# A two-layer adaLN stack: rows gathered by a token table instead of scattered by slot, and every engine in program order

## The chip, the cores and the metric

The kernel runs on one core of a Trainium2 chip. Its time is the device time in microseconds (us) of one execution; before the change the median of nine runs is 735.34 us (732.69 to 738.86). The profile is of one further execution. The core's engines run side by side, each through its own queue of instructions: PE (matrix products, and PEld, its weight loads), DVE and ACT (elementwise work, reductions, activations), POOL (elementwise work and all indirect DMAs here) and SP (which here only starts DMAs). They wait for each other by semaphores.

## The reference

8 sequences of 256 tokens with 128 channels, float32, go through two layers of adaptive layer norm. In each layer a token mixer and a mixture of experts are added to x, each with its own shift, scale and gate for each sequence:

```python
h = _layernorm(x) * (1 + ca) + sa
x = x + ga * attn(h)          # layer 0: retention, layer 1: softmax attention
h = _layernorm(x) * (1 + cb) + sb
x = x + gb * ffn(h)           # both: 8 experts, each token goes to 2
```

Layer 0's mixer is retention: causal scores with a decay for each head, 16 heads of 8 channels, rotary positions, a group norm over the channels of a head and all positions of a sequence, and a silu gate. Its experts are relu(x W1 + b1) W2 + b2, with 512 hidden channels. Layer 1's mixer is softmax attention within chunks of 256 tokens, which is one sequence. Its experts are (silu(x G) * (x U)) D. The two chosen experts' outputs are weighted by a softmax over their two router logits.

## The kernel before

**Tiling.** The 2048 tokens are 4 groups of 512 (`G`, `NTL` = 4 tiles of 128 tokens), resident in SBUF as `xg[g]`. The mixers work group by group and chunk by chunk: `retention` (L581) for layer 0, `Attention` (L767, `run` L973) for layer 1. The experts work on halves of two groups: 1024 tokens, `HT` = 8 tiles. With two choices for each token there are 2048 rows, which are sorted by expert into `NS` = 23 blocks of 128 slots; each expert's rows begin at a block's first slot, so that every block has one expert and some slots are empty.

**A half's way through the experts.** `route` (L343) normalises x into `hm` (`modulated_norm`, DVE L268, POOL L277 and L278), forms router logits on PE, takes the top two on DVE, counts the tokens of each expert by a triangular product (pc, L395) and so obtains for each token and choice its slot (`slot`, L426) and for each block its expert (`ex`). It then writes the 16 tiles of rows (8 tiles, two choices) to a DRAM buffer `xs` at their slots: 16 indirect DMAs on POOL (L447), each of 128 rows of 512 bytes. `xs` has 23 × 128 rows and is filled with zeros at the start by two DMAs (L110), since empty slots are read too. `experts` (L457) reads `xs` back in plain loads of four blocks (`fetch`, L466, on SP's queue), transposes four blocks at a time on PE (`turn`, L469, pt_s L244; ACT copies the result to xT, L474), and for each block loads its expert's weights (`we`, L501, on SP's queue, the expert's number read from `ex` into a register), computes the hidden channels (`hidden0` L741: PE ph, ACT and DVE h; `hidden1` L998: PE pg and pu, ACT sg, DVE h L1010), and one block later the output (`leave`, L477: py on PE L480, DVE copy yr L485). Every four blocks go to the DRAM buffer `ys` by a store on ACT's queue (L488). `combined` (L514) brings each token's two result rows back by two indirect DMAs on POOL (yk, L536; 16 for each half), weights and adds them (ACT L540, DVE L543), in layer 0 adds the b2 term by PE, and `add_gated` (L308) multiplies by the gate on DVE and adds to x on POOL (x L316). After layer 1 a group leaves by a store on SP's queue (L1045).

**Order.** Side work is written as Python generators in a list, `sides`. `tick` (L182) moves each of them on to its next `yield`. The main loops call `tick` two or three times in each block or round, so that routing, combining and the modulation's matmuls are emitted between the main instructions. `tc.manual_schedule(engines={PE})` (L1013) keeps PE's instructions in the order in which they are emitted; the instructions of DVE, ACT, POOL and SP are put in order by a scheduler.

**Which halves meet what.** Routing of half 0 of layer 0 runs beside retention, that of half 1 beside experts(0,0). `combined(0,0)` and the attention's projections run beside experts(0,1), `combined(0,1)` and routing of layer 1's half 0 beside attention, routing of half 1 beside experts(1,0), `combined(1,0)` beside experts(1,1), and `combined(1,1)` alone at the end.

Of the kernel before, what the change touches and what calls it, by code (L numbers as in the profile page):

```python
# [10 lines left out]
FP = mybir.dt.float32  # L11
# [7 lines left out]
P = 128  # L19
# [23 lines left out]
def kernel(  # L43
# [59 lines left out]

    xs, ys = [], []
    zeros = wk.tile([P, P], FP, tag="rs", name="zeros", bufs=1)
    nc.gpsimd.memset(zeros, 0.0)
    for half in range(G // HG):
        xs.append(tc.dram_tile([NS * P, C], FP, name=f"xs{half}"))
        ys.append(tc.dram_tile([NS * P, C], FP, name=f"ys{half}"))
        nc.sync.dma_start(  # L110
            out=xs[half].rearrange("(j p) c -> p j c", p=P),
            in_=zeros.unsqueeze(1).to_broadcast([P, NS, P]),
        )
# [36 lines left out]
                   allow_small_or_imprecise_dtypes=True)  # L150
    slot_no = const.tile([P, NS, NE], FP, tag="slot_no", name="slot_no")
# [34 lines left out]

    def settle():
        while sides:
            tick()


    def modulation(layer, c_sb, wmod_sb, made):
# [13 lines left out]
        scb = wk.tile([P, B, P], FP, tag="hm", name=f"scb{layer}")  # L206
        nc.vector.tensor_copy(scb, sc.unsqueeze(2).to_broadcast([P, B, P]))
# [3 lines left out]
        for b in range(0, B, 2):  # L211
            yield
            pg = bank("sc", f"pg{layer}_{b}")
            for n in range(2):
                nc.tensor.matmul(
                    pg[:, n * 256 : (n + 1) * 256], lhsT=scb[:, b + n, :],
                    rhs=wmod_sb[:, 4:6, :], start=True, stop=True,
                )
# [11 lines left out]
            for n in range(2):  # L230
                nc.tensor.matmul(
                    pr[:, n * 256 : (n + 1) * 256], lhsT=scb[:, b + n, :],
# [21 lines left out]
    def modulated_norm(key, g, mod, shift, scale, got, rows=None, hm=None):  # L254
# [4 lines left out]
        for t in range(NTL):  # L259
            nc.vector.bn_stats(st[:, t, :], xg[g][:, t, :])  # L260
        for t in range(NTL):
            nc.vector.bn_aggr(mv[:, t, :], st[:, t, :])
        rstd = inv_std(key, mv[:, :, 1], NTL)
        yield
        yield
        xn = wk.tile([P, NTL, P], FP, tag="xn", name=f"xn_{key}")
        for t in range(NTL):
            nc.vector.tensor_scalar(  # L268
                xn[:, t, :], xg[g][:, t, :], mv[:, t, 0:1], rstd[:, t : t + 1],
                ALU.subtract, ALU.mult,  # L270
            )
        if rows is not None:
            for n in range(2):
# [5 lines left out]
        yield  # L279
        yield  # L280
# [9 lines left out]
        yield  # L290
# [17 lines left out]
    def add_gated(key, g, gates, which, y):  # L308

        tmp = wk.tile([P, NTL, P], FP, tag="t3", name=f"res_{key}", bufs=1)  # L310
# [32 lines left out]
    def route(layer, half, ready, wr, bias):  # L343
# [6 lines left out]
        hm = wk.tile([P, HT, P], FP, tag="hm", name=f"hm_{key}")  # L350
        lg = sm.tile(sh, FP, tag="lg", name=f"lg_{key}")
        mx = sm.tile(sh, FP, tag="mx", name=f"mx_{key}")
        mi = sm.tile(sh, U32, tag="mi", name=f"mi_{key}")
        for u in range(HG):
# [5 lines left out]
            yield from modulated_norm(f"{key}_{u}", g, mod, SB, CB, got, rows, hm[:, tiles, :])  # L360
# [3 lines left out]
            for t in range(NTL):  # L364
                nc.tensor.matmul(
                    pv[:, t, :], lhsT=hT[:, t * P : (t + 1) * P], rhs=wr, start=True, stop=True
                )
            if bias is None:
# [18 lines left out]
        both = sm.tile([P, HT + 1, NE], BF, tag="both", name=f"both_{key}")  # L387
        nc.gpsimd.memset(both[:, HT, :], 0.0)
        nc.vector.tensor_tensor(both[:, :HT, :], pick[:, 0], pick[:, 1], ALU.add)
        yield  # L390
        yield
# [8 lines left out]
        pos = sm.tile([P, HT + 1, NE], FP, tag="pos", name=f"pos_{key}")  # L400
        nc.vector.tensor_copy(pos, pc)

        big = sm.tile([P, NE, NE], FP, tag="big", name=f"big_{key}")
# [10 lines left out]
        at_slot = sm.tile(sh, FP, tag="lg", name=f"as_{key}")  # L414
# [12 lines left out]

        past = wk.tile([1, NS, NE], FP, tag="past", name=f"past_{key}", bufs=1)
# [7 lines left out]
        w = sm.tile([P, 4, HT], FP, tag="w2", name=f"w2_{key}")  # L436
        d, e = w[:, 2, :], w[:, 3, :]
        nc.vector.tensor_tensor(d, mx[:, :, 1], mx[:, :, 0], ALU.subtract)
        nc.scalar.activation(e, d, AF.Exp)
        nc.vector.tensor_scalar(d, e, 1.0, None, ALU.add)  # L440
        nc.vector.reciprocal(w[:, 0, :], d)
        nc.vector.tensor_tensor(w[:, 1, :], e, w[:, 0, :], ALU.mult)
        own = []
        for t in range(HT):
            yield
            for k in range(2):
                inst = nc.gpsimd.indirect_dma_start(  # L447
                    out=xs[half][:, :],
                    out_offset=bass.IndirectOffsetOnAxis(ap=slot[:, k, t : t + 1], axis=0),
                    in_=hm[:, t, :], in_offset=None,  # L450
                )
                for other in own:
                    tc.declare_no_dep(inst.ins, other, reason="no two choices share a slot")
                own.append(inst.ins)
        routed[layer, half] = (slot, w, pick, ex)

    def experts(layer, half, blob, width, hidden):  # L457


        _, _, _, ex = routed[layer, half]  # L460
        xs_view, ys_view = (a[half].rearrange("(j p) c -> p j c", p=P) for a in (xs, ys))

        def fetch(q):
            n = min(NTL, NS - q)
            xr = wk.tile([P, NTL, P], FP, tag="xr", name=f"xr_{layer}_{half}_{q}", bufs=3)
            nc.sync.dma_start(out=xr[:, :n, :], in_=xs_view[:, q : q + n, :])  # L466
            return xr

        def turn(q, xr):  # L469
# [683 lines left out]
```

## Time and profile before

| what | value |
|---|---|
| median of nine runs | 735.34 us |
| profiled execution | 733.37 us |
| its span, first to last instruction | 731.7 us |
| mean granted TensorE clock | 0.855 |
| DMA, mean over the span | 122 GB/s, 89.22 MB |
| retention (0 to 131.4 us) | PE busy 98.84 us |
| experts(0,0) (144.7 to 236) | PE busy 73.22 us |
| experts(0,1) (236 to 325) | PE busy 67.62 us |
| attention (325 to 521) | PE busy 155.01 us |
| experts(1,0) (521 to 611) | PE busy 77.24 us |
| experts(1,1) (611 to 698.5) | PE busy 69.52 us |

The page has the busy time of each engine; the span in 40 slices, in which a digit is the busy share in tenths, PEclk the granted clock of PE in tenths of full speed; DMA queues; the chain of work that ended last; and groups of instructions by line, with their count, busy time, mean duration and the idle time of the engine ahead of them, by what ended it (`<-`). Views of the trace give the same for chosen windows, the waits by pair, and a timeline of single instructions. In a name such as `yk_c<-ys,slot_r` the output stands first, then the inputs.

### The profile page before, as it was taken

Reading aid. Unit: us, or ns where it says so; the run is one execution under the profiler, and the core shown is the slowest. Engines: PE = TensorE matmul, PEld = TensorE weight load, DVE = VectorE, ACT = ScalarE, POOL = GpSimd, SP = SyncE. Lnnn points to the kernel's source line nnn. Section 1 sums busy time; section 2 is a strip of 40 time slices with the busy share of each in tenths; the row PEclk is TensorE's granted clock in tenths of the full one; section 3 lists DMA queues with packets and bytes.
Section 4 is the critical chain, followed back from the end, with each engine's and each line's share of the span. In section 5 each row is a group of like instructions: output and inputs, shape, how many; then the busy total and the mean of one; then the engine's idle time right before and its main releaser. Section 6 shows DMA issues by size and latency. Waiting matters only on the chain.

```text
span 731.7 us, 12589 instructions
## 1 busy us (share of the span) xinstructions
PE 541.5 (74%) x4608; PEld 407.6 (56%) x4608; DVE 340.5 (47%) x1053; ACT 225.7 (31%) x495; POOL 296.5 (41%) x418
## 2 busy tenths in 40 slices
PE   3899784197588589938786997858997697489910
PEld 2555452096587567814443453425797697479910
DVE  5566665264233476423767576825362231233311
ACT  1553341142123342423352443412441121212201
POOL 5457466835305430065335136475126202600045
PEclk9999897589698799965898798966998799599975
DMA  8300004256585246610000000430176598378712
GB/s 239 98 22 1 2 1 138 79 172 219 172 267 164 85 144 183 204 44 25 1 2 1 1 3 1 147 127 3 46 259 236 194 299 296 96 248 303 260 36 61
DMA packets 53902, 89.22 MB, mean 122 GB/s; under 512 B 5576, under 2 KB 39248, under 8 KB 53840
## 3 DMA queue, kind: packets, MB, share of 16 engines
q1 hardware_dynamic: 37584, 73.99, 31.3%
q0 software_dynamic: 4096, 8.40, 3.8%
q10 hardware_dynamic: 12160, 6.03, 2.8%
q8 instruction: 36, 0.59, 0.3%
q14 instruction: 26, 0.21, 0.1%
HBM read 74.11 MB, written 14.29 MB: 121 GB/s over the span
## 4 chain that ended last, share of the span: by engine, by line
PE 41%; DVE 15%; POOL 14%; DMA 14%; issue 10%; another core or an unknown queue 3%; ACT 2%; SPq 0%; POOLq 0%; ACTq 0%; DVEq 0%
DMA we<-in_l_ew_dram 8%; PE py L480 8%; DVE nm L850 5%; POOL yk_c L536 4%; PE pg L1003 4%; PE sm L844 4%; PE ph L747 4%; PE pu L1003 4%; DMA yk_c<-ys,slot_r 2%; DMA ys<-yr 2%; POOL xs L447 2%; PE sm L836 2%; PE pn L939 2%; POOL x L316 2%
## 5 line engine op out<-in xcount | busy, mean ns | idle before, releaser
L480 PE MATMUL py<-we,h 128*128 128x128 f32 x736 | 105.9, 290 | 27.4 <-DVE h L1010 14.6
L536 POOL DMA_INDIRECT yk_c<-ys,slot_r x64 | 61.3, 958 | 157.1 <-DMA ys<-yr 136.9
L480 PEld LDWEIGHTS py<-we,h 128*128 128x128 f32 x736 | 96.5, 204 | 33.2 <-DVE h L1010 15.3
L447 POOL DMA_INDIRECT xs<-hm_r,slot_r x64 | 62.5, 977 | 47.6 <-DVE slot_r L426 30.3
L850 DVE TENSOR_REDUCE nm<-sm 128x4 f32<-128x512 f32 x96 | 60.2, 680 | 17.7 <-PE sm L844 17.4
L1010 DVE TENSOR_TENSOR h<-pu,sg 128x512 f32<-128x512 f32 x46 | 31.7, 689 | 78.0 <-PE pu L1003 58.3
L903 ACT ACTIVATE e<-se 128x512 f32<-128x512 f32 x96 | 49.9, 600 | 55.1 <-PE se L897 50.2
L320 POOL TENSOR_SCALAR_AFFINE_SELECT e<-e 128x512 f32<-128x512 f32 x64 | 39.7, 643 | 59.9 <-ACT e L903 59.8
L1003 PE MATMUL pg<-xT,we 128*128 128x128 f32 x368 | 52.8, 289 | 11.9 <-DMA we<-in_l_ew_dram 5.6
L747 PE MATMUL ph<-xT,we 128*128 128x128 f32 x368 | 54.0, 294 | 6.7 <-DMA we<-in_l_ew_dram 3.4
L1003 PEld LDWEIGHTS pg<-xT,we 128*128 128x128 f32 x368 | 47.2, 201 | 15.1 <-ACT xT L474 6.6
L1008 ACT ACTIVATE sg<-pg 128x512 f32<-128x512 f32 x46 | 27.4, 596 | 90.5 <-PE pg L1003 72.4
L747 PEld LDWEIGHTS ph<-xT,we 128*128 128x128 f32 x368 | 49.0, 206 | 10.6 <-DMA we<-in_l_ew_dram 5.2
L1003 PE MATMUL pu<-xT,we 128*128 128x128 f32 x368 | 51.8, 285 | 0.5 <-issue 0.3
L755 DVE TENSOR_SCALAR h<-ph,we 128x128 f32<-128x128 f32 x92 | 28.2, 344 | 46.6 <-ACT h L753 16.7
L753 ACT ACTIVATE h<-ph,we 128x128 f32<-128x128 f32 x92 | 28.7, 365 | 68.5 <-PE ph L747 30.9
L1003 PEld LDWEIGHTS pu<-xT,we 128*128 128x128 f32 x368 | 47.6, 202 | 0.9 <-issue 0.9
L543 DVE SCALAR_TENSOR_TENSOR acc_c<-yk_c,w_r,acc_c 128x128 f32<-128x128 f32 x32 | 11.2, 351 | 77.1 <-DMA yk_c<-ys,slot_r 74.8
L844 PE MATMUL sm<-kz,qs_a 32*128 32x512 f32 x192 | 40.4, 745 | 0.0
L485 DVE COPY yr<-py 128x128 f32<-128x128 f32 x92 | 26.5, 288 | 27.6 <-PE py L480 14.6
L540 ACT ACTIVATE acc_c<-yk_c,w_r 128x128 f32<-128x128 f32 x32 | 12.9, 402 | 77.0 <-DMA yk_c<-ys,slot_r 73.4
L320 POOL TENSOR_SCALAR_AFFINE_SELECT a<-a 128x512 f32<-128x512 f32 x32 | 20.6, 658 | 25.6 <-ACT a L648 25.6
(199 smaller groups left out, 932.9 us busy)
## 6 DMA issues: line engine op xcount, KB each, us to landing
we<-in_l_ew_dram SPq DMA_DIRECT2D x46, 768.0 KB
we<-in_l_ew_dram SPq DMA_DIRECT2D x46, 514.0 KB
xr<-xs SPq DMA_DIRECT2D x20, 256.0 KB
ys<-yr ACTq DMA_DIRECT2D x20, 256.0 KB
xs<-zeros SPq DMA_DIRECT2D x2, 1472.0 KB
x<-in_x_in_dram SPq DMA_DIRECT2D x4, 256.0 KB
xs<-hm_r,slot_r POOLq DMA_INDIRECT x64
yk_c<-ys,slot_r POOLq DMA_INDIRECT x64
```

The costliest lines, as they stand in the source:

```text
L320: nc.gpsimd.affine_select(out=src, in_=src, compare_op=ALU.is_ge, fill=0.0, base=0, pattern=[[0, 4], [1, P]], channel_multiplier=-1,)
L447: inst = nc.gpsimd.indirect_dma_start(out=xs[half][:, :], out_offset=bass.IndirectOffsetOnAxis(ap=slot[:, k, t : t + 1], axis=0), in_=hm[: ...
L480: nc.tensor.matmul(py, lhsT=h[:, fc, :], rhs=we[:, width - FF + fc * C : width - FF + (fc + 1) * C], start=(fc == 0), stop=(fc == NFC - 1),)
L536: nc.gpsimd.indirect_dma_start(out=yk[:, k, :], out_offset=None, in_=ys[half][:, :], in_offset=bass.IndirectOffsetOnAxis(ap=slot[:, k, at ...
L747: nc.tensor.matmul(ph[:, i, :], lhsT=we[:, fc * P : (fc + 1) * P], rhs=xT, start=True, stop=True)
L753: nc.scalar.activation(h[:, fc, :], ph[:, i, :], AF.Relu, bias=b1)
L755: nc.vector.tensor_scalar(h[:, fc, :], ph[:, i, :], b1, 0.0, ALU.add, ALU.max)
L844: nc.tensor.matmul(scs[i], lhsT=qs[part, t0 : t0 + P], rhs=kz[part, :, k * P : (k + 1) * P], start=(k != c), stop=True,)
L850: nc.vector.tensor_reduce(nm[:, 4 * i : 4 * i + 4], scs[i], AX.X, ALU.max, negate=True)
L903: nc.scalar.activation(e, scs[i], AF.Exp)
L1003: nc.tensor.matmul(p[:, fc, :], lhsT=we[:, i * FF + fc * P : i * FF + (fc + 1) * P], rhs=xT, start=True, stop=True,)
L1010: nc.vector.tensor_tensor(h, pu, sg, ALU.mult)
```

## The change

1. *Rows.* `xs` now holds the 1024 tokens in their order (`HT` × 128 rows). `route` stores `hm` there, a plain store of four tiles for each group on POOL's queue. The zero fills are gone. A **token table** says for each slot which token's row belongs there. It is built on chip: the slot is split into a block number (`part[:, 0]`) and a row in the block (`part[:, 1]`); `owner` holds, for each token, choice and block, the token's row and tile number where the token's slot lies in that block, and zero elsewhere (three DVE operations of 128x368); `hot` is, for each tile and choice, a 128x128 bf16 matrix that has a one at the row of the slot (16 DVE operations), and 16 matmuls add `hot`ᵀ × `owner` into `pown` (128x46). Two DVE operations make of it `token` (row + 128 × tile). An empty slot gets token 0.
2. *Gathers.* Each block's rows come by an indirect DMA on POOL from `xs` by `token[:, j]` (23 for each half, 92 in all) in place of the scatters and of `fetch`. For the first half of a layer the first eight are issued in `begun`, one for each stage; later ones one for each block, eight blocks ahead, running over into the first eight of the half that follows.
3. *Order.* `tc.manual_schedule()` without an argument: DVE, ACT, POOL and SP too run in the order in which instructions are emitted. The side generators yield much more often (`hop`), retention ticks four times instead of two or three for each chunk, and attention five times instead of three for each round.
4. *Routing's place.* The routes of both halves of a layer are started together and run side by side (`routing`), with two buffers for several small tiles. `hm` becomes one tile for each group.
5. *Combining.* `combined` begins three stages later. The rows of tile `at` are gathered two tiles ahead of the arithmetic on them, the two gathers in separate stages. `add_gated` multiplies in place there.
6. *Queues.* The out stores move from SP's to POOL's queue. The `ys` stores (still ACT's queue) are issued one step later, after the next block's hidden products. The modulation's broadcast `scb` is made for four sequences at a time.

```diff
-        own = []
-        for t in range(HT):
-            yield
-            for k in range(2):
-                inst = nc.gpsimd.indirect_dma_start(
-                    out=xs[half][:, :],
-                    out_offset=bass.IndirectOffsetOnAxis(ap=slot[:, k, t : t + 1], axis=0),
-                    in_=hm[:, t, :], in_offset=None,
-                )
...
+            nc.gpsimd.dma_start(
+                out=xs[half].rearrange("(u t p) c -> u p t c", p=P, t=NTL)[u], in_=hm
+            )
...
+        nc.vector.tensor_tensor(
+            owner[:, 1], block.unsqueeze(1).unsqueeze(1).to_broadcast(per),
+            part[:, 0].unsqueeze(3).to_broadcast(per), ALU.is_equal,
+        )
+        nc.vector.tensor_scalar(owner[:, 0], owner[:, 1], token_row[:, 0:1], None, ALU.mult)
+        nc.vector.tensor_tensor(
+            owner[:, 1], owner[:, 1], token_tile.unsqueeze(3).to_broadcast(per), ALU.mult
+        )
...
+                    nc.vector.tensor_scalar(
+                        hot, row16, part[:, 1, k, t : t + 1], None, ALU.is_equal
+                    )
...
+                    nc.tensor.matmul(
+                        pown, lhsT=hots[2 * (t - 2) + k], rhs=owner[:, :, k, t - 2, :],
+                        start=(t == 2 and k == 0), stop=(t == HT + 1 and k == 1),
+                    )
...
+    def gather(layer, half, j):
+
+        q, t = j // NTL, j % NTL
...
+        nc.gpsimd.indirect_dma_start(
+            out=raw[layer, half, q][:, t, :], out_offset=None, in_=xs[half][:, :],
+            in_offset=bass.IndirectOffsetOnAxis(ap=token[:, j : j + 1], axis=0),
+        )
...
+    def begun(layer, half):
+
+        for j in range(2 * NTL):
+            gather(layer, half, j)
+            yield
...
-        raw = {0: fetch(0), NTL: fetch(NTL)}
...
+            for _ in range(2):
+                if ahead and ahead[0][:2] in routed and total - len(ahead) <= j:
+                    gather(*ahead.pop(0))
...
             tick()
+            store()
             if last is not None:
                 leave(*last)
             tick()
...
-    with tc.manual_schedule(engines={mybir.EngineType.PE}):
+    with tc.manual_schedule():
...
-            nc.sync.dma_start(out=out_view[g], in_=xg[g])
+            nc.gpsimd.dma_start(out=out_view[g], in_=xg[g])
```

More of the change, by code (lines that the diff above doesn't have):

```diff
@@ L455, in route @@
[L455 to L469, printed above, removed]
-            n = min(NTL, NS - q)
+        per = [P, 2, HT, NS]
@@ L475, in turn @@
             return xT
+        full = []
         def leave(j, we, h, yr):
@@ L508, in experts @@
             tick()
[L509 to L510 removed]
+            if j % NTL == 2 and (q + 1) * NTL < NS:
+                xT[q + 1] = turn(q + 1)
             last = (j, we, h, yr)
         leave(*last)
+        store()
+        for more in ahead:
+            while following not in routed:
+                tick()
+            gather(*more)
     def combined(layer, half, finished):
         key = f"c{layer}_{half}"
[L518 removed]
+        slot, w, pick, _, _ = routed[layer, half]
+        yield from hop(3)
         gates = made[layer][1]
```

264 lines of the change are left out of this document (170 added, 94 removed).

## The prediction, made before the changed kernel had run

> **What bounds the kernel now.** The page's first two parts come first: no engine is full, PE is the fullest.
>
> ```profile
> span 731.7 us, 12589 instructions
> PE 541.5 (74%) x4608; PEld 407.6 (56%) x4608; DVE 340.5 (47%) x1053; ACT 225.7 (31%) x495; POOL 296.5 (41%) x418
> PE   3899784197588589938786997858997697489910
> POOL 5457466835305430065335136475126202600045
> PEclk9999897589698799965898798966998799599975
> ```
>
> Each digit is 18.3 us. PE's digits fall to 1 (slice 8) and about 5 (10, 13, 31), where POOL's rise; its clock falls with its work. So I asked next for busy time by windows around POOL's long runs of indirect DMAs: three of scatters, three of gathers, a stretch of comparison, the boundary before layer 0's experts and the tail.
>
> ```profile
> core 0: us, PE busy (x) PEld busy (x) DVE busy (x) ACT busy (x) POOL busy (x), PEclk, DMA share, GB/s
> 170.40:190.50 20.10, 10.37 (x74) 9.29 (x74) 3.49 (x14) 2.46 (x7) 15.46 (x16) 0.85 0.51 168
> 470.80:488.80 18.00, 8.74 (x74) 4.68 (x74) 5.38 (x13) 1.97 (x5) 14.12 (x15) 0.80 0.49 185
> 551.80:571.90 20.10, 11.22 (x86) 10.23 (x84) 2.16 (x5) 2.38 (x4) 15.49 (x16) 0.79 0.54 183
> 225.00:245.00 20.00, 10.45 (x48) 8.34 (x47) 6.04 (x16) 6.19 (x18) 15.30 (x16) 0.77 0.34 102
> 315.10:336.70 21.60, 9.08 (x60) 4.38 (x58) 5.83 (x16) 4.75 (x11) 17.32 (x19) 0.60 0.17 46
> 616.40:637.50 21.10, 8.35 (x46) 7.57 (x45) 5.14 (x15) 4.65 (x11) 16.64 (x17) 0.62 0.34 109
> 466.00:474.90 8.90, 6.09 (x74) 2.52 (x76) 6.71 (x16) 3.36 (x8) 7.00 (x9) 1.00 0.76 271
> 131.40:144.70 13.30, 0.00 (x0) 0.00 (x0) 3.86 (x11) 0.34 (x1) 11.48 (x15) 0.57 0.24 76
> 698.50:731.70 33.20, 0.00 (x0) 0.00 (x0) 4.65 (x13) 3.21 (x8) 17.89 (x18) 0.57 0.20 54
> ```
>
> In the first six rows, 120.9 us in all, PE works 58.2; its mean over the span is 74%. In 466–475 four indirect DMAs stand about 1.8 us apart and PE keeps 68% at full clock. The timeline of the third row shows how a run stalls PE:
>
> ```profile
> 558.48 1.06 PE L480 MATMUL py<-we,h 128*128 128x128 f32 x8
> 559.51 0.96 POOL L447 DMA_INDIRECT xs<-hm_r,slot_r  x1 [0.30 <-issue]
> 561.73 0.59 ACT L474 COPY xT<-pt_s 128x512 f32<-128x512 f32 x1 [6.40 <-remote]
> 562.37 1.20 PE L1003 MATMUL pg<-xT,we 128*128 128x128 f32 x8 [2.83 <-ACT xT L474]
> 571.70 0.69 DVE L1010 TENSOR_TENSOR h<-pu,sg 128x512 f32<-128x512 f32 x1 [12.51 <-remote]
> 572.45 0.80 PE L480 MATMUL py<-we,h 128*128 128x128 f32 x2 [6.11 <-DVE h L1010]
> ```
>
> ACT and DVE start long after the PE result that they need ("remote": no releaser found), and PE then waits for them. What makes the release late is not shown; that it happens inside unbroken runs of scatters is. Last, waits and groups:
>
> ```profile
> POOL yk_c L536 <- DMA ys<-yr: 136.9, 3, 57.7
> DVE acc_c L543 <- DMA yk_c<-ys,slot_r: 74.8, 28, 8.7
> L536 POOL DMA_INDIRECT yk_c<-ys,slot_r x64 | 61.3, 958 | 157.1 <-DMA ys<-yr 136.9
> ```
>
> POOL is not short of time in all: it waits 137 us for the results' store. What counts is where its runs lie.
>
> **The change, part by part.** The sum is made against the profiled execution, 733.37 us, which is 1.97 below the median of 735.34. A term's bounds follow in brackets.
>
> *Boundary retention → experts(0,0).* PE's gaps there are 13.33 us before pt_s L244 and 5.86 + 1.17 before pr L666 (waiting for POOL L320 behind scatters): 20.4. The 16 scatters go; in their place come a dense store of hm, the table, and 8 gathers, of which four (4 × 1.26, from 0.96 + 0.30 issue) must land before pt_s. Both halves' routes now run here, so group 3's normalisation (POOL rstd 1.05, gsc, yn, o, from the DVE rows at 137.85–139.0) lies in the same chain: about 10 us after the last pr, against 17.0 (127.76 to 144.72). Some 7 to 8 us of gaps remain: gain 13 [0, 16].
>
> *The three scatter runs under work.* From the timelines PE loses 1.78 + 3.38 + 3.73 + 2.13 = 11.0 in the first, 1.25 + 6.23 + 5.6 (eight sm matmuls over 6.69 instead of 1.1) = 13.1 in the second, 2.83 + 0.34 + 6.11 = 9.3 in the third: 33.4. In their place one gather is issued per block of 2.94 us (67.6 us PE over 23 blocks) or 3.7, eight blocks ahead. That is wider than the 1.8 of the stretch at 466. I take 30 [0, 33.4], the nearest row being that one.
>
> *The gather runs of `combined`.* PE loses 2.91 + 2.40 + 4.69 = 10.0, 5.20 + 6.12 = 11.3 and 7.62 + 1.56 + 3.57 = 12.75. There ACT L540 and DVE L543 wait for a gather and the experts' h, xT and yr stand behind them. Two tiles ahead, a landing of about 2.5 us (issue 708.47, reader 711.01) is covered by two ticked stages. In experts(0,1), though, up to three indirect DMAs fall in a block: 3.8 us of POOL against 2.94, over about ten blocks −9. I take 2 [−9, 10] there, 5 [0, 11.3] in attention, where eight gathers no longer run back to back, and 7 [0, 12.75] in experts(1,1).
>
> *All engines in stated order.* PE waits for DVE zmax L866 (23.0 us, 12 times) and oT L946 (11.5, 3 times), where the scheduler put side work ahead on DVE. More ticks cut that work smaller: 8 [0, 16]. The price: DVE's bn_stats stands behind x += L316, POOL, and that now behind gathers; queued behind bn_stats are the experts' h and yr, for which PE waits. 3 [0, 10].
>
> *Clock.* The 58.2 us busy in the six windows ran at a mean clock of 0.74; at full clock 43. With shorter gaps I take 8 [0, 15].
>
> *Table.* Per route on DVE: 3 operations 128x368 and 16 of 128x128 (L485's row 0.288) plus about ten small ones (0.2): 7.5 us; four routes 30, each spread over some twenty stages beside PE's work in retention, attention (DVE 59–60% busy in their windows) and two experts' halves (36–38%). Exposed 5 [0, 30]; cover gone, all 30. PE's 64 pown matmuls: the eight of 128x64 bf16 at pc L395 take 0.35, so 16 with loads under 0.9: 3 for four.
>
> *Queues and tail.* From SP go 24 fetches, the zero fill and four out stores; SP keeps the weights, so nothing that PE waits on moves behind anything. POOL loses 64 × 1.28 = 82 us and gains 92 × 1.26 = 116 plus 12 plain stores, while it is 41% busy; hidden, except for the last out store, priced between an indirect issue and the present store's whole 3.5 (728.2 to 731.7): 1.5 [0, 5].
>
> *Two rules against it.* The longest gather, beside a DVE operation, took 1.13 us at 722.11, against 0.95 for most. The Trainium skill ("DMA: Bandwidth & Descriptors", section "SWDGE vs HWDGE vs iDMA") says that descriptors made on GpSimd go through rings in SBUF from which some VectorE modes lock it out, while transfers from SP are immune: against moving loads to POOL. By the row that is at most 0.18 × 92 = 17 us of POOL, not of PE. The same page's section "Anatomy of one DMA — SWDGE (gpsimd) path" states about 2.0 us fixed per DMA: 92 small gathers for 24 loads would by it be some 136 us more if nothing overlapped (an estimate), but gathers at 707.21–714.72 follow each other at 1.26 while each lands 2.5 later.
>
> Sum: 13 + 30 + 2 + 5 + 7 + 8 + 8 = 73 gained, 3 + 5 + 3 + 1.5 = 12.5 lost, net −60.5: 672.9, at the median **675**.
>
> **Rivals.** *B1, POOL binds where three streams meet.* For: POOL's digits 6–8 at each run, and x +=, rstd and hm share its queue. Experts(0,1) loses 9 instead of gaining 2, the other two gather runs keep their 12, in-order waits cost 10 instead of 3: +30, **705**. Against: POOL's 41%.
>
> *B2, slower: the late release belongs to each software DMA, not to the run.* For: both kinds of run show it, and no row names its cause. PE lost 67.4 us to 96 such DMAs under work, 0.70 each; afterwards some 150 lie under work (92 gathers + 48 + 10 stores), 105. With the boundary, order and costs as above: 733.4 + 37.6 − 13 − 8 + 12.5 + 2 = **764**. It decides above 75.9/150 = 0.51 us each. Against: 466–475, four DMAs without a lag.
>
> *B3, the eight-block lead doesn't hold:* POOL reaches the gathers of blocks 8–11 late because route(0,1)'s hm and stores are ahead of them in its order, and turn(2) waits in each half: 4 × 4 us, **690**. For: the second half's table is built in the first half's blocks.
>
> *B4, the waits moved but nothing else:* the order's loss equals its gain, **735**.
>
> **How the numbers follow.** Forecast 0.54, B1 0.19, B3 0.05, B2 0.20, B4 0.02. The forecast's own range is 655 to 695. Low end of the range: gains 103 of their upper 114.5, costs 4: 636. High end: half the gains taken (36.5), costs 39: 738; above lies B2. The measurement tells a change from none at about 0.3% (2.2 us): faster 0.54 + 0.19 + 0.05 = 0.78, same 0.02, slower 0.20.
>
> **What would show it.** Right: no PE gap over 3 us in the experts' stages with POOL at even pitch; a pt_s wait under 8 us at the first boundary; no "remote" wait over 3 us; clock above 0.88. Wrong in the table: DVE over 375 us busy with PE behind it. B1: PE waiting for DVE h in experts(0,1) while DVE waits for POOL x L316. B2: remote waits in every block. B3: pt_s waiting for gathers at each third block. What I can't price is the late release itself; if it follows anything but the runs, the forecast falls.

## The result: 6 per cent slower, and the profile after

The changed kernel took 781.14 us (median of ten runs, 775.88 to 790.50) against 734.99 for the kernel before on the same chip: a ratio of 1.062, with a 95% interval of 1.059 to 1.065. The forecast was 675. The profiled execution has a span of 782.1 us against 731.7.

From the page of the changed kernel: the span, the busy times, and three of the rows of 40 slices (19.6 us each here).

```profile
span 782.1 us, 12860 instructions
PE 562.7 (72%) x4672; PEld 420.5 (54%) x4672; DVE 365.9 (47%) x1155; ACT 225.4 (29%) x497; POOL 331.5 (42%) x462
PE   4677566576767757898789778787788799587900
POOL 4323544527724343521873723327427040663063
PEclk9996768655969779799989988689999899799965
```

Before, PE's first seven digits were 3 8 9 9 7 8 4, now the first nine are 4 6 7 7 5 6 6 5 7: the loss is at the start. The later stages look much as before. Cutting both traces at the same instructions gives the stages (us; retention ends with the last pr, the boundary with the first ph; experts(0,0) and (1,0) end at half of the matmuls ph and pg, (0,1) at the last ph, attention at the first pg, experts(1,1) at the last py):

| | retention | boundary | experts(0,0) | experts(0,1) | attention | experts(1,0) | experts(1,1) | tail | span |
|---|---|---|---|---|---|---|---|---|---|
| before | 127.8 | 18.8 | 69.2 | 94.3 | 211.8 | 82.9 | 93.6 | 33.4 | 731.7 |
| after | 176.9 | 13.5 | 69.0 | 103.1 | 207.5 | 83.4 | 90.6 | 38.2 | 782.1 |
| difference | +49.1 | −5.3 | −0.2 | +8.8 | −4.3 | +0.5 | −3.0 | +4.8 | +50.4 |

**Retention holds nearly the whole loss**; the other stages change by −5.3 to +8.8 and come to +1.3 together. Busy time by windows, first of the kernel before, then of the changed one:

```profile
core 0: us, PE busy (x) PEld busy (x) DVE busy (x) ACT busy (x) POOL busy (x), PEclk, DMA share, GB/s
0.00:127.80 127.80, 96.09 (x876) 57.92 (x876) 77.64 (x249) 46.41 (x103) 73.92 (x133) 0.91 0.24 72
```

```profile
core 0: us, PE busy (x) PEld busy (x) DVE busy (x) ACT busy (x) POOL busy (x), PEclk, DMA share, GB/s
0.00:176.90 176.90, 114.06 (x892) 65.46 (x892) 87.49 (x279) 46.44 (x102) 70.41 (x129) 0.77 0.12 36
```

PE has 16 matmuls more, but is busy 18 us longer, at a mean clock of 0.77 instead of 0.91; its idle time grows by 31 us (62.8 against 31.7). No engine is fuller than before in share: DVE falls from 61% to 49%, POOL from 58% to 40%. A stage in which every engine is idler and which takes longer is one in which they wait for each other in turn. The waits say where; from the view of waits of the changed kernel, 20 to 177 us (time waited in all, times, longest):

```profile
ACT a L748 <- PE rs L736: 50.0, 14, 8.5
PEld rs L736 <- POOL rz L348: 28.4, 6, 6.4
DVE a L744 <- PE rs L736: 27.0, 11, 4.7
POOL qa L679 <- DVE qa L675: 26.7, 3, 11.5
PE rs L736 <- POOL rz L348: 23.7, 6, 6.1
```

In the kernel before, PE's rs never waits for rz there. The chain of waits in the changed kernel shows why it does now (start, duration, what):

```profile
89.29 0.89 PE pp_a L317 x8
...
91.09 0.67 DVE res_a L328 x2
91.84 1.30 POOL x L331
93.16 0.87 DVE lnst_r L274 x4
...
94.60 1.03 POOL rstd_r L265
95.65 0.61 DVE xn_r L283 x2
96.34 0.73 POOL hm_r L291
97.14 0.72 POOL hm_r L292
97.86 0.92 POOL rz L348 x2
98.82 2.09 PE rs L736 x8
```

The end of group 0's retention (res, x) and the norm of its routing (lnst_r, rstd_r, xn_r, hm_r) are side work that nobody needs soon. But POOL's rz, which makes the next row's operand, is emitted behind hm_r, so PE's rs at 98.82 waits for a chain that leads from engine to engine, over 9 us from pp_a. In the kernel before, the scheduler had put rz ahead of them. POOL's lines of its timeline at the same place, the end of group 0:

```profile
58.89 1.26 POOL L578 TENSOR_TENSOR qa<-qa,qa 128x512 f32<-128x512 f32 x1 [1.98 <-DVE qa L574]
60.26 1.85 POOL L333 TENSOR_SCALAR rz<-qa,cols 128x256 f32<-128x256 f32 x4
...
63.90 1.27 POOL L316 TENSOR_TENSOR x<-x,res_a 128x512 f32<-128x512 f32 x1
...
68.83 0.76 POOL L277 TENSOR_TENSOR hm_r<-xn_r,rows 128x256 f32<-128x256 f32 x1 [0.72 <-DVE xn_r L268]
```

PE's pieces in such a chain run at a lower clock: four pqa matmuls take 3.80 us at 74.37, where the granted clock is 0.50, and their mean over the kernel is 978 ns against 740 before. (The Trainium skill, "TensorE: Matmul & The Clock Gate", section "Part 1: The HAM clock gate", states that the clock follows how busy PE has been of late and is half or full; the fall from 0.91 to 0.77 over a stage with more gaps agrees.)

**The runs of indirect DMAs are still there.** The prediction had them replaced by one gather in each block. From the timeline of the changed kernel in experts(0,0):

```profile
208.81 0.60 PE L258 MATMUL pt_s<-ident,xr 128*128 128x128 f32 x4
...
212.47 0.94 POOL L520 DMA_INDIRECT xr<-xs,token_r  x1 [0.30 <-issue]
213.14 0.58 ACT L544 COPY xT<-pt_s 128x512 f32<-128x512 f32 x1 [4.80 <-remote]
213.72 0.94 POOL L520 DMA_INDIRECT xr<-xs,token_r  x1 [0.30 <-issue]
...
217.47 0.94 POOL L520 DMA_INDIRECT xr<-xs,token_r  x1 [0.30 <-issue]
219.55 0.61 DVE L859 TENSOR_SCALAR h<-ph,we 128x128 f32<-128x128 f32 x2 [6.84 <-remote]
222.76 0.71 PE L497 MATMUL pown_r<-owner_r,hot_r 128*128 128x46 bf16 x4 [7.82 <-DVE hot_r L489]
232.23 0.94 POOL L520 DMA_INDIRECT xr<-xs,token_r  x1 [13.82 <-PE pt_s L258]
```

Gathers follow each other at 1.25 us as the scatters did. The number in brackets is the engine's idle time before the line: ACT and DVE again stood idle, for 4.8 and 6.8 us, without a releaser, and took PE's results 3.7 and 4.6 us after PE's last matmul on them (pt_s ended at 209.41, ph at 214.94). Such a wait of over 2 us without a releaser is called a late release below. Since DVE's order is fixed, hot stands behind the late h and PE's pown waits 7.8 us for it. Then POOL waits 13.8 us for a free xr buffer. Program order says which gather comes after which. It doesn't say when: POOL runs ahead until the three xr buffers are full, and after each wait issues what has piled up. Counting DMAs of POOL that start within 1.6 us of each other, the changed kernel has runs of 13, 12, 11 and 12 at 203, 269, 591 and 664 us.

### The profile page after: what moved, and what is told of

Same layout as the page of the kernel before. It is cut to its first block, busy times and chain, and to the rows that moved or that the text cites. A ratio compares the mean times of both kernels' runs of the same rounds, so it can differ in the third digit from the quotient of the medians.

```text
span 782.1 us, 12860 instructions
## 1 busy us (share of the span) xinstructions
PE 562.7 (72%) x4672; PEld 420.5 (54%) x4672; DVE 365.9 (47%) x1155; ACT 225.4 (29%) x497; POOL 331.5 (42%) x462
## 4 chain that ended last, share of the span: by engine, by line
PE 42%; DVE 18%; POOL 14%; issue 11%; DMA 7%; another core or an unknown queue 4%; ACT 3%; ACTq 0%; POOLq 0%; SPq 0%; DVEq 0%
PE py L552 6%; DMA we<-in_l_ew_dram 4%; POOL yk_c L625 4%; PE pg L1111 4%; DVE nm L954 4%; PE pu L1111 4%; PE sm L948 3%; PE ph L851 3%; PE rs L736 2%; PE se L1001 2%; DMA yk_c<-ys,slot_r 2%; POOL xr L520 2%; PE pqa L309 2%; PE pn L1043 2%
## 5 line engine op out<-in xcount | busy, mean ns | idle before, releaser
L520 POOL DMA_INDIRECT xr<-xs,token_r x92 | 88.4, 960 | 81.8 <-PE pt_s L258 31.2
L625 POOL DMA_INDIRECT yk_c<-ys,slot_r x64 | 61.5, 960 | 96.1 <-DMA ys<-yr 49.2
L1118 DVE TENSOR_TENSOR h<-pu,sg 128x512 f32<-128x512 f32 x46 | 31.7, 690 | 103.3 <-PE pu L1111 62.2
L851 PE MATMUL ph<-xT,we 128*128 128x128 f32 x368 | 56.3, 302 | 8.7 <-issue 4.0
L851 PEld LDWEIGHTS ph<-xT,we 128*128 128x128 f32 x368 | 50.9, 213 | 13.0 <-issue 7.5
L736 PE MATMUL rs<-rz,ka 32*128 32x512 f32 x128 | 24.4, 842 | 26.2 <-POOL rz L348 23.7
L948 PE MATMUL sm<-kz,qs_a 32*128 32x512 f32 x192 | 35.3, 726 | 3.8 <-DVE oT_a L1051 3.8
L1026 PEld LDWEIGHTS yd<-e,vz 128*32 128x32 f32 x768 | 22.2, 118 | 23.3 <-issue 19.0
L748 ACT COPY a<-rs 128x512 f32<-128x512 f32 x32 | 17.2, 591 | 56.7 <-PE rs L736 50.0
```

What stands on the lines that cost most here:

```text
L520: nc.gpsimd.indirect_dma_start(out=raw[layer, half, q][:, t, :], out_offset=None, in_=xs[half][:, :], in_offset=bass.IndirectOffsetOnAxis( ...
L625: nc.gpsimd.indirect_dma_start(out=yk[:, k, :], out_offset=None, in_=ys[half][:, :], in_offset=bass.IndirectOffsetOnAxis(ap=slot[:, k, at ...
L736: nc.tensor.matmul(sc, lhsT=kr[part, t0 : t0 + P], rhs=z[part, :, c * P : (c + 1) * P], start=True, stop=True,)
L851: nc.tensor.matmul(ph[:, i, :], lhsT=we[:, fc * P : (fc + 1) * P], rhs=xT, start=True, stop=True)
L948: nc.tensor.matmul(scs[i], lhsT=qs[part, t0 : t0 + P], rhs=kz[part, :, k * P : (k + 1) * P], start=(k != c), stop=True,)
L1118: nc.vector.tensor_tensor(h, pu, sg, ALU.mult)
```

## The experiments

Eighteen runs followed, on several chips. The kernel before took 735 to 738 us on three of them (called A here; the first result is from one), and 720 to 722 on two (called B). Each ratio is to the kernel before on the same chip, with its 95% interval. Stages as in the table above.

**1 to 4: order, and the place of rz (chip B).**

e1_pe_only, from the changed kernel; e2_ret_sched has this line up to the end of retention and the removed one again behind it:

```diff
-    with tc.manual_schedule():
+    with tc.manual_schedule(engines={mybir.EngineType.PE}):
```

e3_before_pda, from the kernel before:

```diff
-    with tc.manual_schedule(engines={mybir.EngineType.PE}):
+    with tc.manual_schedule(engines={mybir.EngineType.PE, mybir.EngineType.DVE, mybir.EngineType.Activation}):
```

e4_place_early, from the changed kernel, in retention's loop; `ready_place()` calls `place(at + 1)` once, as soon as c is 1 and the next row's group is there:

```diff
                 as_ = scores(at, c)
-                tick()
-                tick()
+                ready_place()
+                for _ in range(2):
+                    tick()
+                    ready_place()
...
-                tick()
-                tick()
+                for _ in range(2):
+                    tick()
+                    ready_place()
```

> The changed kernel with only PE held to the order of emission, the other engines left to the scheduler as before. In the changed kernel the last pr of retention ends at 176.9 us, before the change at 127.8; the other stages together differ by 1 us. Theory 1 (the fixed order of DVE, ACT and POOL costs the 49 us): retention ends at 125 to 140, the whole at 725 to 745. Theory 2 (PE's own order has changed with the finer stages, the extra ticks and the two routes side by side, and this costs the 49): PE's order is the same here as in the changed kernel, so retention ends at 165 or later, the whole at 770 or more.

> The changed kernel with the fixed order of all engines only from the end of retention on; during retention only PE is held to it. Theory 1: retention ends at 125 to 140 and the whole comes to 730 to 745, since the later stages stay as in the changed kernel (781 less 36 to 49). Theory 2: 770 or more. Against the run with PE alone fixed throughout it tells what the fixed order is worth in the later stages: the same within 5 us if it is worth nothing there, lower by 8 if the term of the prediction for the order holds.

> The kernel before the change with PE, DVE and ACT held to the order of emission (POOL and SP left to the scheduler, since the scatters could not keep their freedom from each other in a fixed order); nothing else changed. Theory 1: retention, which emits its side work there in coarser pieces than after the change, grows by 25 to 50 us, the whole to 760 to 790. Theory 2: it stays within 10 us, 730 to 745.

> The changed kernel with one move in retention: the operations that make the next row's rz (two on ACT, two on POOL, and the copies into vz) are emitted as soon as the next row's group is there, ahead of the stages of side work instead of behind them. In the changed kernel PE's weight loads wait 28.4 us for POOL rz, six times. If it is mainly this that stands behind side work in the fixed order, retention ends at 150 to 157 and the whole comes to 755 to 762. If the loss is spread over every step of the chain (DVE a, hT, qa, x), it is worth 10 us or less: 771 or more.

| run | ratio | retention | boundary | attention | span |
|---|---|---|---|---|---|
| e1_pe_only | 1.0315 [1.025, 1.038] | 143.9 | 18.9 | 226.3 | 744.9 |
| e2_ret_sched | 0.981 [0.975, 0.987] | 144.6 | 12.9 | 204.9 | 706.7 |
| e3_before_pda | 0.983 [0.978, 0.989] | 139.7 | 12.7 | 184.5 | 701.7 |
| e4_place_early | 1.004 [1.001, 1.007] | 156.4 | 13.5 | 201.6 | 720.2 |

Neither theory is right alone. The scheduler gives retention back 32 of its 49 us (176.9 to 144.6), but not the other 17, and PE's order is the same in both: so the fixed order costs about 32 and the rest must lie in PE's own order and in the added side work. The single move of rz gives back 20.5 of it. The waits of e4 over 20 to 175 us show that it was this step:

```profile
PEld rs L736 <- POOL rz L348: 7.9, 3, 2.8
PE rs L736 <- POOL rz L348: 7.1, 3, 2.6
```

Outside retention the fixed order is a gain, and a large one: from the last pr to the end e1 takes 601.0 us and e2 562.1, with the same instructions. Of those 39 us attention has 21. The kernel before gains 1.7% from the order of DVE and ACT alone (e3): its retention is 139.7 (127.8 in the first profile, on another chip), so it grew by 12 and not by the 25 to 50 expected of theory 1; that it has less side work there and that POOL stayed free may be why, which no run shows. From the last pr on, e3 takes 562.0 us, as much as e2 with the whole change in it (562.1). e2 is 25 us shorter in the four experts' halves together (306.2 against 331.2) and about as much longer in attention (204.9 against 184.5) and the tail (38.0 against 33.6). So on this chip the gathers show no net gain over an order of DVE and ACT alone; what in the change costs attention its 20 us wasn't separated.

**5 to 8: the chip, POOL's order, the ticks (chip A).**

b2_before and a2_after are unchanged copies. e7_after_pda is the changed kernel with e3's line. e8_old_ticks, from e4_place_early, first in retention, then in attention:

```diff
-                for _ in range(2):
-                    tick()
-                    ready_place()
+                tick()
+                ready_place()
...
-                for _ in range(2):
+                for _ in range(2 - c):
...
                     es = self.weights(at, c, k)
-                    tick()
...
                     tick()
-                    tick()
```

> The kernel before the change once more, unchanged, for its profile on the chip on which the three kernels after it run. In the last four runs the kernel before took 720.2 us on their chip, against 735.0 earlier, and none of the four showed a release of ACT or DVE by PE that comes over 2 us late without a releaser, while both first profiles show several. If these late releases belong to the chip and not to the kernel, this profile has none where the time is about 720, and some where it is about 735.

> The changed kernel once more, unchanged, beside the kernel before on the same chip. If the late releases belong to the chip and cost both kernels about the same (15 us before), the ratio stays at 1.06 and retention is again some 45 to 50 us longer, the other stages together about even. If spacing the indirect DMAs does hide what the late releases cost, the ratio is higher here than 1.062 where the chip shows none, since only the kernel before has something to gain from their absence.

> The changed kernel with PE, DVE and ACT held to the order of emission and POOL and SP left to the scheduler: the setting in which the kernel before took 0.983 of its time. If POOL's fixed order is what costs (rz, qa and x += behind hm, stores and gathers that wait), this gives back 30 us or more: ratio 1.02 or less, retention under 155 us. If it is the order of DVE and ACT, or PE's own, 1.045 or more.

> The changed kernel with the earlier place of the rz operations (ratio 1.004 on its chip) and with the old number of ticks: in retention three and two for the two chunks instead of four each, in attention three in each round instead of five. If the extra ticks crowd side work into the chain of the main loops, the ratio falls to 0.985 or below. If the finer stages need them, the side work now ends later and the loops that wait for it (the next group's projection, the first gathers) take it back: 1.00 to 1.03.

| run | ratio | retention | boundary | span |
|---|---|---|---|---|
| b2_before | – | 130.9 | 18.8 | 737.8 |
| a2_after | 1.0615 [1.052, 1.071] | 176.6 | 13.5 | 785.9 |
| e7_after_pda | 1.033 [1.023, 1.043] | 162.8 | 17.1 | 760.7 |
| e8_old_ticks | 1.017 [1.009, 1.025] | 126.4 | 34.4 | 750.8 |

The late releases go with the chip: b2_before, at 739 us, shows six, a2_after thirteen, in the same stretches as the first profiles. The changed kernel's retention doesn't depend on the chip (176.9 and 176.6 on chips A, 177.2 in e16 below on a chip B); that of the kernel before, 127.8 and 130.9, was profiled on chips A alone. Freeing POOL and SP alone gives 14 us of retention back. With the old number of ticks and rz early, retention is as short as before the change, but 21 us of it come back at the boundary, where the routes that were not done are finished with PE idle: the extra ticks had spread that work into the main loop's chain; without them it is left over.

**9 to 12: what is left over, a best version, the table, the gathers (chip B).**

e9_route_later, from e8_old_ticks:

```diff
-        for half in range(2):
-            sides.append(routing(half, 0, kept, wg_sb, None))
+        sides.append(routing(0, 0, kept, wg_sb, None))
         retention(range(G), made[0][0], kept.add)
         while 0 not in ahead:
             tick()
+        sides.append(routing(1, 0, kept, wg_sb, None))
```

e12_best, from e9_route_later, with e2's lines and

```diff
-            nc.gpsimd.dma_start(out=out_view[g], in_=xg[g])
+            nc.sync.dma_start(out=out_view[g], in_=xg[g])
```

e10_no_table, from the changed kernel, without row, part, owner, hot and pown, and with

```diff
+        nc.vector.tensor_scalar(token, block, token_row[:, 0:1], None, ALU.add)
```

e11_loads_sp, from the changed kernel, in `gather`:

```diff
-        nc.gpsimd.indirect_dma_start(
...
+        if t == 0:
+            nc.sync.dma_start(
+                out=raw[layer, half, q][:, :n, :],
+                in_=xs[half].rearrange("(j p) c -> p j c", p=P)[:, (q % 2) * NTL : (q % 2) * NTL + n, :],
+            )
```

> The kernel of the run before with the old ticks and the earlier rz (retention 126.4 us, boundary to the first ph 34.4, ratio 1.017), with the second half's route of layer 0 started after retention, as before the change, instead of beside it. If it is the second route that fills retention's engines and is left over at its end, the boundary falls to 13 to 19 us with retention at 120 to 128 and the ratio to 0.985 to 1.00. If the boundary is long because of the first route's own finer stages, it stays over 28 and the ratio at 1.01 or more.

> That kernel with the scheduler's order (PE alone fixed) during retention, the fixed order of all engines after it, and the out stores on SP's queue again. From the parts: retention 125 to 135, boundary about 14, the tail 34 instead of 38, the stages between as in the changed kernel: ratio 0.95 to 0.98, faster than both kernels. If the fixed order of the later stages is worth nothing without what retention leaves to them, 0.99 to 1.01.

> The changed kernel without the token table: row, part, owner, the 64 hot matrices and the 64 pown matmuls are left out, and token is filled from two constants, so that the gathers read rows of other tokens; the number of stages is the same. The prediction put 8 us on the table (5 on DVE, 3 on PE); then the ratio to the kernel before is about 1.05 where the changed kernel has 1.062. If the table is what crowds retention's order (pown waited 15.6 us for hot), it is 1.03 or less; if it is hidden, 1.058 or more.

> The changed kernel with the 92 gathers left out: each xr tile of four blocks comes by one plain load on SP's queue from rows of xs that are not those of its slots. All else, the table too, stays. On a chip with late releases (before about 735): if each indirect DMA costs PE 0.2 us or more whatever its spacing, this gives back 20 us or more, ratio 1.035 or less, and the releases over 2 us late stay only at the gathers of combined; if only unbroken runs cost, 8 to 15, since the changed kernel still has runs of up to ten. Where the chip shows none: 5 us or less.

| run | ratio | retention | boundary | experts(0,0) | experts(0,1) | attention | experts(1,0) | experts(1,1) | tail |
|---|---|---|---|---|---|---|---|---|---|
| e9_route_later | 0.981 [0.976, 0.987] | 126.4 | 24.7 | 62.5 | 86.1 | 204.2 | 76.4 | 85.2 | 37.9 |
| e12_best | 0.981 [0.975, 0.987] | 115.5 | 24.0 | 63.2 | 89.3 | 201.2 | 75.9 | 98.2 | 35.1 |
| e10_no_table | 0.990 [0.987, 0.993] | 168.7 | 15.6 | 54.6 | 85.9 | 202.4 | 70.1 | 81.6 | 37.9 |
| e11_loads_sp | 1.013 [1.009, 1.016] | 175.1 | 13.0 | 60.3 | 89.5 | 201.7 | 76.1 | 71.1 | 37.7 |

With the second route out of the way the boundary falls from 34.4 to 24.7, not to the 13 to 19 expected. The total gets below the kernel before in the fixed order of all engines (0.981); but e8 ran on a chip A and e9 on a chip B, so of the step from 1.017 only the 10 us at the boundary can be put down to the route. The table is worth 20 to 25 us on this chip, not 8: 8 in retention (176.9 to 168.7), 6 to 9 in experts(0,0) and 6 to 8 in experts(1,0), against the other kernels of chip B that share these stages (60.3 to 63.2 and 75.9 to 77.7). The gathers, with the wait for their table, cost some 13 us on chip B: from the last pr on e11 takes 549.4 us, e2 and e4 562.1 and 563.8, and most of it lies in experts(1,1), 71.1 against 80.5 to 85.2 (e2, e4, e9, e10).

e12 has a loss of its own in experts(1,1). From its timeline, SP's and PE's lines:

```profile
601.92 1.27 POOL L331 TENSOR_TENSOR x<-x,acc_c 128x512 f32<-128x512 f32 x1
603.22 0.40 SPq L1166 DMA_DIRECT2D out_dram<-x  x1
604.83 2.67 SPq L581 DMA_DIRECT2D we<-in_l_ew_dram  x3
609.58 2.04 PE L1116 MATMUL pg<-xT,we 128*128 128x128 f32 x8 [14.64 <-DMA we<-in_l_ew_dram]
```

In the fixed order SP holds the store of a finished group until x is there, and the next blocks' weight loads stand behind it: three go out together at 604.8, and PE waits 14.6 us; with a second wait of 8.5 this makes 23. In e9, which differs in this store and in retention's order and ran on the same chip, experts(1,1) is 13 us shorter (85.2 against 98.2) and the tail 2.8 longer. The change had moved these stores to POOL, so that SP had nothing but weights.

**13 to 16: both kernels and two parts on one chip (chip A).** b3_before and a3_after are unchanged copies; e14_best_pool is e12 with the out stores on POOL again; e11_b_loads_sp is e11 once more.

> The kernel before the change, unchanged, for its profile on this call's chip. Where it takes about 720 us, no release over 2 us late stands in its trace, and its six runs of indirect DMAs leave PE smaller gaps; where about 735, they stand there.

> The changed kernel, unchanged. On a chip without late releases: retention 175 as elsewhere, the stages after it as in the run with retention alone left to the scheduler (562 us from the last pr on), together 737 to 742, ratio 1.02 to 1.03; that would say that the change suffers more from late releases than the kernel before. If the ratio is 1.06 there too, retention's loss is set against nothing gained later. On a chip with them: 1.06 as twice before.

> The version that beat both kernels, with the out stores back on POOL's queue as in the change: with them on SP's queue PE waited 14.6 and 8.5 us for weights in the last experts' half, since in the fixed order SP's next weight loads stand behind a store that waits for x. If that is the cause, that half takes 84 to 88 us instead of 98.2, the tail 38 instead of 35, and the ratio falls from 0.981 to 0.965 to 0.97. If not, it stays at 0.98.

> The changed kernel without the 92 gathers (plain loads of other rows on SP's queue), beside the changed kernel on one chip. Without late releases it was at ratio 1.013, with 71.1 us in the last half and the other stages within 1 to 3 us of their values in the other runs: 12 to 16 us below the changed kernel. On a chip with late releases: 20 us or more below it if each gather costs PE something, 8 to 15 if only unbroken runs do.

| run | ratio | retention | boundary | experts(0,0) | experts(0,1) | attention | experts(1,0) | experts(1,1) | tail |
|---|---|---|---|---|---|---|---|---|---|
| b3_before | – | 127.2 | 18.7 | 70.0 | 95.1 | 213.7 | 83.7 | 92.7 | 33.4 |
| a3_after | 1.068 [1.063, 1.073] | 176.8 | 13.5 | 67.3 | 102.2 | 212.0 | 83.3 | 93.6 | 38.1 |
| e14_best_pool | 0.985 [0.981, 0.988] | 117.0 | 23.8 | 69.5 | 95.5 | 203.3 | 85.0 | 91.9 | 37.9 |
| e11_b_loads_sp | 1.006 [1.003, 1.010] | 176.2 | 13.0 | 61.5 | 91.6 | 201.9 | 75.0 | 77.0 | 37.5 |

The gathers cost 45 us on this chip (medians of 787.5 and 742.8), 0.49 for each of the 92. (The profiled execution of e11_b, 735.5, is among the faster ones of its ten.) Two of these windows of a3_after, then of e11_b_loads_sp:

```profile
core 0: us, PE busy (x) PEld busy (x) DVE busy (x) ACT busy (x) POOL busy (x), PEclk, DMA share, GB/s
190.30:257.60 67.30, 52.59 (x410) 49.25 (x411) 32.11 (x139) 19.16 (x55) 33.93 (x41) 0.89 0.70 203
571.90:655.20 83.30, 73.31 (x602) 70.88 (x603) 35.43 (x119) 20.70 (x33) 27.09 (x30) 0.94 0.72 227
```

```profile
core 0: us, PE busy (x) PEld busy (x) DVE busy (x) ACT busy (x) POOL busy (x), PEclk, DMA share, GB/s
189.30:250.80 61.50, 52.12 (x410) 49.16 (x411) 32.60 (x139) 19.15 (x55) 8.88 (x15) 0.93 0.74 223
544.30:619.30 75.00, 69.64 (x602) 68.33 (x603) 35.47 (x119) 20.93 (x33) 6.05 (x7) 0.95 0.75 245
```

PE, DVE and ACT execute the same instructions. Only POOL has lost its gathers, and PE's idle time falls from 14.7 and 10.0 us to 9.4 and 5.4. In e11_b there is one late release (3.5 us), in a3_after ten. The stages of e11_b are those that the kernels have on chip B. The out stores back on POOL gave e14 91.9 in experts(1,1); the 84 to 88 expected was for a chip B, and this chip was A. At 0.985 it beats both kernels here.

**17 and 18: gathers tied to their blocks (chip B).**

```diff
             q = j // NTL
+            if j >= 2:
+                pace = sm.tile([1, 1], FP, tag="pace", name=f"pace_{layer}_{half}_{j}")
+                nc.gpsimd.tensor_copy(pace, left[j - 2])
```

Here `left[j]` is one element of the row that block j's output was copied to.

> The changed kernel with one small POOL copy added ahead of each block's gather from the third block on: it reads the result that the block two before has left, so that POOL can't run ahead and issue gathers in a row; their number stays 92. Where the chip has late releases (before 735 to 738): if unbroken runs cost, experts(0,0) falls from 67 to 69 us to 61 to 63, experts(1,0) from 83 to 75 to 77, and the ratio from 1.062 to 1.068 to 1.03 to 1.05; if each indirect DMA costs whatever its spacing, nothing moves, 1.06 or more. Where it has none (before 720): no effect within 4 us of 740, ratio 1.02 to 1.03.

> The version with retention by the scheduler, the old ticks, the second route later and the out stores on POOL (ratio 0.985 on a chip with late releases), with the same pacing. If unbroken runs cost: 0.95 to 0.97 on a chip with late releases; where there are none 0.955 to 0.965, pacing being worth nothing there. If each DMA costs: 0.985.

e16 is at 1.046 [1.043, 1.050] (754.4 us), e17 at 0.972 [0.967, 0.977] (703.3). Both ran on a chip B, without late releases, so the question that they were made for stays open: whether each gather costs or only runs of them. On this chip pacing is no gain: e16 is 14 us above the 740 that I had estimated for the unpaced kernel, and its experts(1,0) take 79.9 against 75.9 to 77.7 in the unpaced kernels. e17, for which 0.955 to 0.965 was expected, is the best ratio of the study; e12 with POOL stores wasn't run on a chip B, so pacing has no share in it that is shown.

## Why the prediction was wrong

**The step that failed: "All engines in stated order"**, a gain of 8 and a price of 3 [0, 10]. The price was worked out for one wait, bn_stats behind x += in the experts, and the question "what is queued behind it" was never put to retention, whose 131 us the prediction did not open. There it costs about 32 of the 49 us (e2), 20 of them in one place, rz behind hm_r (e4). The other 17 are left with the scheduler's order too; extra ticks, the second route and the table (8, e10) are what the runs name for them, without a share for each. With old ticks, a later second route and the scheduler, retention falls to 115 to 119 us (e12, e14, e17). What spoke for it was in the trace before: in retention DVE and POOL were 61% and 58% busy, and PE waited 8.1 us for POOL's a.

**The gain of order elsewhere was undersized**: 8 taken, [0, 16]; 39 measured after retention (e1 against e2, chip B).

**"The three scatter runs", 30 [0, 33.4]: nothing came.** Experts(0,0), attention and experts(1,0) changed by −0.2, −4.3 and +0.5 on the first chip. The argument was "one gather per block of 2.94 us or 3.7", wider than a stretch of 1.8 without stalls; the trace has runs of 11 to 13 at 1.25. In the two experts' halves the new gathers took back what the scatters had cost. Of the signs that were to show the forecast right, "no remote wait over 3 us" failed eleven times and the clock was 0.843.

**Rival B2 (764 us) has a share.** Its price for each DMA was 0.70, its break-even 0.51, and 0.49 was measured per gather on a chip A, where the kernel without the block gathers is at 1.006 and with them at 1.068. So on chips A two costs of nearly the same size stand side by side, retention's 49 us and the gathers' 45, and without either one the changed kernel is about even with the kernel before (measured for the gathers, an estimate for retention: 781 less 49). On chips B the gathers cost some 13 us, retention is as long, and the estimate below is still 1.03. That B2's sum is the nearest to the time is in part luck: it holds nothing for retention.

**Gather runs of combined:** 2, 5 and 7 taken; experts(0,1) lost 8.8, near rival B1's 9 and at its place (POOL issues without a pause from 269 to 284 us, while a late h holds DVE and PE waits 8.7 us for scb behind it); attention gained 4.3 in all, experts(1,1) 3.0.

**Boundary:** from the last pr to pt_s 17.0 became 11.8; "about 10" was forecast. The term's other part, the gaps before pr, can't be told apart inside the new retention. **Clock:** 8 taken; the mean fell from 0.855 to 0.843, by retention's 0.77. **Table:** 8 taken [3, 33], 20 to 25 measured on chip B. The DVE operations were cheaper than the row that I took (hot 252 ns, the three owner operations 0.52, 0.32 and 0.54 us), but PE in its fixed order waits for hot, 15.6 us in six waits. **Tail:** 1.5 [0, 5] taken, 4.8 measured. **Queues:** that SP's weights move behind nothing was right, and e12 shows what the old place of the stores would cost under a fixed order: 23 us in two waits for weights, 13 us of the half.

**The two rules weighed against it** did not decide. The Trainium skill's rule on lockout, in "DMA: Bandwidth & Descriptors", section "SWDGE vs HWDGE vs iDMA", would show, if anywhere in this trace, as longer issues on POOL: the 92 gathers took 960 ns in the mean, the 64 scatters before 977. Of the 2 us fixed per DMA nothing was seen as such, since gathers overlap; what they cost showed as idle time of PE, on chips A together with late releases.

## What to carry to other kernels

Before all engines are put in program order, read each stage for the operation that the next main step needs (rz here) and emit it ahead of side work; keep the scheduler for a stage whose order you haven't written out. The order is not a clock: an engine that is ahead issues everything that its buffers allow, so a stream that should be spaced has to wait for something that is spaced (whether spacing pays wasn't shown: on a chip B it didn't). And under a fixed order a queue with urgent loads must hold no store that waits for a result. The order also pays by itself: the kernel before gained 1.7% from fixing DVE and ACT alone, on a chip B.

## What was not expected of the hardware

ACT and DVE stood idle for up to 15 us before they took a result of PE, without a releaser in the trace, beside runs of indirect DMAs, on some chips and not on others. In all ten profiles from chips where the kernel before took 735 to 738 us there is such a wait of over 2 us, in none of the ten from chips where it took 720 to 722, though kernels there have runs as long (13, 12, 11 and 18 in e2). The changed kernel lost 45 us to its gathers on such a chip. Why chips differ in this isn't settled. The changed kernel has no unpaced run on a chip B; its retention, 176.9, and the later stages of e2 or e4, 562.1 or 563.8, make a span of 739 to 741 us, which against the 720 of the kernel before there is a ratio of about 1.03 (an estimate). By it, if the chips differ in nothing else, the late releases account for about half of the loss on the first chip. That they differ in nothing else isn't shown: the kernel without block gathers, with one late release in its profile on chip A, takes 742.8 us there and 730.2 on chip B.
